# A graph network on one Trainium2 core: node tiles in edge order five quarter steps later, the first block of edges ahead of the order checks, and all source one-hots of the first stage on ScalarE

## The chip, the cores and the metric

The kernel runs on one core of a Trainium2 chip. A core has five engines with instruction queues of their own: PE (TensorE, matrix products; the profile shows its weight loads apart, as PEld), DVE (VectorE), ACT (ScalarE), POOL (GpSimd) and SP (SyncE, which issues DMAs here). The metric is the device time of one execution in microseconds. The kernel before took 5880.89 us (median of 3 runs, 5874.62 to 5888.94).

## The reference

There are 12,500 nodes with 96 features and 200,000 edges, sorted by destination. Four layers follow each other, each with a residual and a layer norm:

- layer 0: `x @ W_self + (mean over incoming edges of x[src]) @ W_neigh + b`
- layer 1, twice: `concat(x @ W1 + b1, sum over incoming edges of (x @ W0 + b0)[src]) @ W2 + b2`, divided by the row's standard deviation
- layer 2: attention per edge with 8 heads, `exp(clip(sum(K[src] * Q[dst] * E)))`, where E comes from 96 features of the edge itself, and a weighted mean of `V[src]`
- layer 3: a softmax over incoming edges of `relu(x[src])`, the weighted sum, and a product with W

So the core of the work is done four times without attention (layer 0, layer 1 twice, layer 3): take a row of a node table for each edge's source, and sum the rows by destination.

## The kernel before

The nodes make 98 tiles of 128 (NB). The edges, in their given order, make 1563 edge tiles of 128. Since the edges are sorted, each node tile draws its edges from a short stretch of some 32 edge tiles. A check in the kernel falls back to a general version if the data don't fit; it plays no part here.

**Two ways to sum.** For the first NS = 72 node tiles (60 in layer 3, NS3) the edges are rearranged: for a destination tile `d`, each edge gets a place by its source tile, 25 granules of 128 places (SQ). The rows of a granule are taken from the node table, which stays in SBUF, by four matmuls against a one-hot by source (`ohT`, L1366; L1231 in the first stage), copied out of PSUM as `msg` (L1369; L1235), and summed by a matmul with a one-hot by destination (`ohd`, L1375; L1244). For the other node tiles (26, or 38 in layer 3) the edges stay in their order: POOL fetches their rows from DRAM with indirect DMAs of 128 rows, one for each edge tile (L1311 in `by_edges`), and PE sums them with a one-hot over 32 edge tiles (L1297). A few edges per node tile that found no place go to two spare granules, whose rows POOL fetches as well (L1175, L1184). In the text an *item* is one granule of one node tile, so a pass over 72 node tiles has 1800 items.

**Stages in time** (us in the profile): a prologue to about 75; the node tables of layer 0 and the first block of edges to about 250; the first stage to 1636, in which the places are worked out, the one-hots made and stored, and layer 0 summed, all together; two passes of layer 1 to 2257 and to about 2900; attention to 4985; the pass of layer 3 to the end.

**The prologue and the first stage.** `edge_constants` makes constants and then checks the order of the edges: first and last destination of each edge tile (`c.first`, `c.cont`, `c.same`), and whether edges are out of order (`c.loose`). `edge_block` loads a block of 128 edge tiles (BL) and works out a few columns per edge; its last value, `b.lead`, compares with `c.first`. `edge_steps` takes 64 edge tiles at a time (GE): a scan per 16 edge tiles counts edges of the same source tile (L1018), a product and 16 small matmuls collect the counts (L1022, L1024), and then one-hots A and R and 64 matmuls put the edges in their places (L1076 to L1097). `l0_nodes` makes the table of layer 0 in 25 batches. `first_sums` is a generator that `passes` resumes: at its step for tile `d` it asks for the places as a row over all partitions (`ask_row`, `bc`), makes the one-hots by source (`one_hots`, L1143 to L1156) and by destination (`destinations`, L1137), fetches the spare rows, and runs the items of the tile. Odd tiles have their source one-hots made by ACT, a square and a ReLU on halves; even tiles by DVE, one comparison.

**A pass** (`whole_pass`) goes through the items in order, ten (or five) at a time: gather on PE, copies on ACT and DVE, then the sums of the ten before. Between them it resumes `by_edges` by quarter steps, four for each node tile in edge order. How often is set by one line (L1390):

```
while made * len(items) < i * 4 * (NB - ns):
    next(others)
    made += 1
```

Inside, each quarter step asks POOL for the rows of edge tiles up to 16 units of four ahead (13 in layer 3), and the first quarter step of the next node tile sums the one before (`take`):

```
while at < min(4 * d - 9 + k + deep, units):
    ...
if k == (3 if count else 0) and d > ns:
    take(d - 1)
```

The first quarter step of a pass therefore asks for nine units, 36 edge tiles, at once. The spare rows of two node tiles are fetched by one more DMA on the same POOL queue, four node tiles ahead (`ask_spares`).

**What sets the order.** Outside attention a planner orders each engine's instructions when the kernel is built, from the program's order and its own costs; an engine then works through its list in order. In attention the order is written out by hand. So where the text says "built order", it means the list of instructions on an engine as the built kernel has it.

Of the kernel before, what the change touches and what calls it, by code (L numbers as in the profile page):

```python
# [11 lines left out]
F32 = mybir.dt.float32  # L12
# [3 lines left out]
AF = mybir.ActivationFunctionType  # L16
ALU = mybir.AluOpType
AX = mybir.AxisListType
PSUM = bass.MemoryType.PSUM
# [4 lines left out]
P = 128  # L24
# [6 lines left out]
NB = 98  # L31
# [487 lines left out]
SD = SQ * P  # L519
# [3 lines left out]
BL = 128  # L523
# [18 lines left out]
def gnn_fast(  # L542
# [4 lines left out]
    nc = tc.nc  # L547
# [12 lines left out]
    pcol1 = const.tile([P, 1], F32, name="pcol1")  # L560
    nc.vector.tensor_scalar(pcol1, pcol, 1.0, None, op0=ALU.add)
    less = const.tile([P, 1], F32, name="less")
# [73 lines left out]
    with tc.tile_pool(name="w_work", bufs=2) as work, tc.tile_pool(name="w_psum", bufs=2, space=PSUM) as psum:  # L636
        for i in range(DEPTH):
            t = const.tile([D + 1, 2 * D], F32, name=f"w_l1_{i}")
            for k, (w, b) in enumerate(((W1[i], b1[i]), (W0[i], b0[i]))):
# [3 lines left out]
                c = work.tile([D, D], F32, name="wc")  # L643
# [187 lines left out]
    def edge_constants(big):  # L831
        c = Edges()
# [17 lines left out]
        c.run = None  # L850
        c.placed = []
        c.blocks = {}
        with tc.tile_pool(name="s_ord", bufs=1) as ordp, tc.tile_pool(name="s_ordp", bufs=2, space=PSUM) as psum:
            ones_f = ordp.tile([P, P], F32, name="ones_f")
            nc.vector.memset(ones_f, 1.0)
# [23 lines left out]
            for j0 in range(0, NT, 512):  # L879
                n = min(512, NT - j0)  # L880
# [10 lines left out]
            o = ordp.tile([P, 2, rw], I32, name="o")  # L891
# [14 lines left out]
            p = psum.tile([P, 512], F32, name="p")  # L906
            nc.tensor.matmul(p[:, :1], ones_f, c.loose, start=True, stop=True)
            nc.vector.tensor_scalar(c.loose, p[:, :1], 0.5, None, op0=ALU.is_ge)
        return c

    def edge_block(c, blk, psum, b0):

        nb = min(BL, NT - b0)
# [42 lines left out]
        b = c.blocks[b0] = Edges()  # L956
# [4 lines left out]
        nc.vector.tensor_copy(col, p[:, : 2 * P].rearrange("p (k t) -> p k t", k=2))  # L961
        hi_i = blk.tile([P, 2, BL], I32, name="hi_i", bufs=1)
        nc.vector.tensor_scalar(hi_i, col, 7, None, op0=ALU.arith_shift_right)
        hi = blk.tile([P, 2, BL], F32, name="hi", bufs=1)
        nc.vector.tensor_copy(hi, hi_i)
        b.shi = blk.tile([P, BL], BF16, name="shi")
        nc.vector.tensor_copy(b.shi, hi[:, 0, :])
# [25 lines left out]
        nc.vector.tensor_add(b.j, b.j, q)  # L993
        b.more = blk.tile([P, BL], F32, name="more")
        nc.vector.tensor_scalar(b.more, q, -1.0, float(SQ - 1), op0=ALU.mult, op1=ALU.add)
        b.lead = blk.tile([P, BL], F32, name="lead")
        nc.vector.tensor_tensor(b.lead[:, :nb], hi[:, 1, :nb], c.first[:, b0 : b0 + nb], op=ALU.is_equal)

    def edge_steps(c, work, psum, t0):

# [2 lines left out]
        b = c.blocks[t0 - c0]  # L1003

        pr = psum.tile([P, 3, GE], F32, name="pr")
        for i0 in range(0, n2, CH):
            n = min(CH, n2 - i0)
# [19 lines left out]
        n = n2  # L1027
# [18 lines left out]
        cs = slice(c0, c0 + n)  # L1046
        at = small("at_")
        nc.vector.tensor_mul(at, full[:, :n], c.cont[:, t0 : t0 + n])
        nc.vector.tensor_mul(at, at, b.lead[:, cs])
        nc.vector.tensor_add(at, at, pr[:, 1, :n])  # L1050
        none = small("none")
        nc.vector.scalar_tensor_tensor(none, at, float(SPARE), ovf, op0=ALU.is_ge, op1=ALU.mult)
# [91 lines left out]
    def one_hots(work, d, bc):  # L1144

        o = work.tile([P, SD], FP8, name="ohT0", bufs=2)
        if d % 2:

            for c in range(0, SD, SD // 2):
                b = bc[:, c : c + SD // 2]  # L1150
                nc.scalar.activation(b, b, AF.Square, bias=less)
                nc.scalar.activation(o[:, c : c + SD // 2], b, AF.Relu, bias=1.0, scale=-1.0, saturate=False)
        else:
            nc.vector.tensor_scalar(o, bc, pcol1, None, op0=ALU.is_equal, saturate=False)
        nc.sync.dma_start(ohT_d[d], o)
        return o  # L1156

# [167 lines left out]
    def whole_pass(of, table, done, rest_done, at=None):  # L1325

        ns = of[0]
        W = table.shape[1]
        R = 4 * D // W
        items = [(d, q) for d in range(ns) for q in range(SQ)]  # L1330
        got, acc = {}, {}
        with ExitStack() as c2:
            tabp = c2.enter_context(tc.tile_pool(name="e_tab", bufs=1))
            work = c2.enter_context(tc.tile_pool(name="e_work", bufs=2))
            msgp = c2.enter_context(tc.tile_pool(name="e_msg", bufs=4))
            psum = c2.enter_context(tc.tile_pool(name="e_psum", bufs=1, space=PSUM))
            at = at or load_table(tabp, table)
            sp = {}

            def ask_spares(d):  # L1340
                if d < ns:
                    sp[d] = sp[d + 1] = gather_spares(tabp, table, d)

            ask_spares(0)
            ask_spares(2)
            others = by_edges(of, msgp, psum, work, table, rest_done, 16 if W == 2 * D else 13)
            next(others)
            made = 0

            def fetch(d):  # L1350
                if d < ns:
                    if d % 2 == 0:
                        ask_spares(d + 4)
                    got[d] = reload(work, d)

            def gather(now, banks, engine):

                n = len(now) // R
                ps = psum.tile([P, n, 512], F32, name=f"rows{n}", bufs=n)
                m = msgp.tile([P, n, R * W], F16, name=f"msg{n}")  # L1360
                for i, (d, q) in enumerate(now):
                    if q == 0:
                        fetch(d + 1)
                    for j in range(NG):
                        a, b = granule(at, got[d][0], sp[d], q, j, d % 2)
                        nc.tensor.matmul(  # L1366
                            ps[j * GR : (j + 1) * GR, i // R, i % R * W : (i % R + 1) * W], a, b, start=True, stop=True
                        )
                (nc.scalar.copy if engine else nc.vector.tensor_copy)(m, ps[:, :, : R * W])  # L1369
                return [(d, q, m[:, i // R, i % R * W : (i % R + 1) * W]) for i, (d, q) in enumerate(now)]  # L1370

            def scatter(d, q, m):
                if q == 0:
                    acc[d] = psum.tile([P, 512], F32, name="acc", bufs=2)
                nc.tensor.matmul(acc[d][:, :W], got[d][1][:, q, :], m, start=(q == 0), stop=(q == SQ - 1))  # L1375
                if q == SQ - 1:
                    done(work, psum, d, acc.pop(d))
                    got.pop(d)
                    sp.pop(d)

            fetch(0)
            waiting = []
            for i in range(0, len(items), 5 * R):
                now = []
                for b0, b1, scalar in ((0, 1, True), (1, 3, True), (3, 5, False)):
                    now += gather(items[i + b0 * R : i + b1 * R], b1 - b0, scalar)
                for w in waiting:
                    scatter(*w)
                waiting = now
                while made * len(items) < i * 4 * (NB - ns):  # L1390
                    next(others)
                    made += 1
            for w in waiting:
                scatter(*w)
            for _ in others:
                pass
# [360 lines left out]
    def passes():  # L1757
        with ExitStack() as c1:
# [8 lines left out]
            nc.scalar.dma_start(q_d[:QM], none[:QM])  # L1767
            nc.scalar.dma_start(q_d[QM + NB * P :], none[: P - QM])
            with ExitStack() as c2:
                tabp = c2.enter_context(tc.tile_pool(name="f_tab", bufs=1))  # L1770
                spare["ring"] = spares(tabp, 2 * D, F16, "spare")
                blk = c2.enter_context(tc.tile_pool(name="s_blk", bufs=2))
                step = c2.enter_context(tc.tile_pool(name="s_work", bufs=2))
                work = c2.enter_context(tc.tile_pool(name="f_work", bufs=1))
                msgp = c2.enter_context(tc.tile_pool(name="f_msg", bufs=2))
                psum = c2.enter_context(tc.tile_pool(name="f_psum", bufs=1, space=PSUM))
                pieces, at = new_table(tabp, 2 * D, F16)
                nodes = l0_nodes(work, psum, pieces)
                sums = first_sums(work, msgp, psum, at, tabs_d[0], c.placed, in_batches(l0_stage, count=True))
                next(sums)  # L1780
                others = by_edges(
                    rest, msgp, psum, work, tabs_d[0], in_batches(l0_stage, count=True, name="sums_e"), 11, count=True
                )
                made = 0
                turn = 1 - AHEAD
                for k, t0 in enumerate(range(0, TS, GE)):
                    if t0 == 0:
                        edge_block(c, blk, psum, 0)
                    if t0 % BL == 0 and t0 + BL < TS:
                        edge_block(c, blk, psum, t0 + BL)  # L1790
                    edge_steps(c, step, psum, t0)
                    for _ in range(26):
                        next(nodes, None)

                    while turn <= min(4 * k, NS - 2):
                        next(sums)
                        turn += 1
                        while made * NS <= turn * 4 * (NB - NS):
                            next(others)
                            made += 1  # L1800
                for _ in sums:
                    pass
                for _ in others:
                    pass
                for b0 in range(-(-TS // BL) * BL, NT, BL):
                    edge_block(c, blk, psum, b0)
# [85 lines left out]
```

## Time and profile before

| | |
|---|---|
| median of the runs | 5880.89 us |
| the profiled execution, its own time | 5885.37 us |
| its span, first to last instruction | 5883.6 us |
| PE busy | 4446.7 us (76%), granted clock 0.749 on the mean |
| DVE busy | 4378.5 us (74%) |
| ACT busy | 2718.9 us (46%) |
| POOL busy | 4095.9 us (70%) |
| moved by DMA | 920.46 MB, 156 GB/s |

A busy time is the share of the span in which an engine had an instruction at work; issuing a DMA isn't counted, except for POOL's indirect DMAs. An average over the span mixes stages with different limits, so the views that matter are those by stage and in a window. In a row of a timeline the columns are start, duration, engine, line and operation, and in brackets the idle time before it and what ended it. In a row of waits: who waited for what, us in total, how often, the longest.

### The profile page before, as it was taken

The page shows a single profiled execution, that of the slowest core. Times are in us where ns is not written, and L with a number is a line of the kernel's source. Part 1 is how long each engine was busy: PE and PEld are TensorE (multiplying, and loading weights), DVE is VectorE, ACT ScalarE, POOL GpSimd, SP SyncE. Part 2 cuts the span into 40 slices and gives each one's busy share as a digit, 9 for nine tenths or more (in the row PEclk, how much of TensorE's full clock was granted, in tenths as well). Part 3 has the DMA queues.
Part 4 walks back from the last instruction along what each step waited for, and adds up shares of the span by engine and source line. Part 5 has one row for each costly group of instructions (what it writes and reads, how often), then busy time and mean ns, then how long its engine had stood idle before and what let it go on. Part 6 is the DMA issues. An engine that isn't in the chain of part 4 may idle for free. (4 is left out here: it accounts for less than half of the span.)

```text
span 5883.6 us, 131235 instructions
## 1 busy us (share of the span) xinstructions
PE 4446.7 (76%) x51487; PEld 3267.7 (56%) x51487; DVE 4378.5 (74%) x9063; ACT 2718.9 (46%) x5380; POOL 4095.9 (70%) x3648
## 2 busy tenths in 40 slices
PE   4667777777778987898666667666666765899998
PEld 3444444554456765666566566666666664445454
DVE  7589899998746665776677777777777777577776
ACT  1445444444534443555444444444444444444444
POOL 0267677767667775777477777777777776777773
PEclk7576767776779998999755655555556566899999
DMA  3555555555556665776555555555555554555553
GB/s 100 156 156 184 172 170 173 164 166 166 179 149 167 171 160 140 190 193 187 150 152 155 157 156 156 156 156 155 156 153 156 155 157 131 137 145 151 146 151 88
DMA packets 671708, 920.46 MB, mean 156 GB/s; under 512 B 399034, under 2 KB 465293, under 8 KB 671077
## 3 DMA queue, kind: packets, MB, share of 16 engines
q1 hardware_dynamic: 502198, 621.59, 33.7%
q0 software_dynamic: 150624, 283.99, 20.8%
q10 hardware_dynamic: 18255, 6.39, 0.5%
q8 instruction: 406, 6.65, 0.5%
q14 instruction: 225, 1.84, 0.1%
HBM read 778.75 MB, written 132.81 MB: 155 GB/s over the span
## 5 line engine op out<-in xcount | busy, mean ns | idle before, releaser
L1311 POOL DMA_INDIRECT rows_e<-tab_d,cols x1257 | 1658.3, 1319 | 423.7 <-issue 292.9
L1536 POOL DMA_INDIRECT kv<-kv_d,cols x1563 | 1590.9, 1018 | 485.4 <-issue 382.0
L1369 ACT CAST msg<-rows 128x768 f16<-128x768 f32 (+1 forms) x1320 | 796.9, 640 | 853.8 <-PE rows L1366 832.8
L1629 PE MATMUL acc<-mh,ohe 128*128 128x208 f16 x3115 | 566.7, 355 | 661.3 <-DVE ohe L1613 653.8
L1369 DVE CAST msg<-rows 128x768 f16<-128x768 f32 x660 | 630.0, 955 | 369.5 <-PE rows L1366 363.6
L1629 PEld LDWEIGHTS <-ohe 128*128 128x128 bf16 x3115 | 379.3, 137 | 781.8 <-DVE ohe L1613 738.4
L1366 PE MATMUL rows<-tab,ohT 128*32 128x192 f16 (+1 forms) x19992 | 763.8, 277 | 56.0 <-ACT msg L1369 21.7
L1311 POOL DMA_INDIRECT rows_e<-ex_d,cols x611 | 592.2, 969 | 186.2 <-issue 154.2
L1375 PE MATMUL acc<-msg,ohd 128*128 128x192 f16 (+1 forms) x5100 | 693.7, 276 | 1.6 <-issue 1.6
L1574 PE MATMUL ep<-w_e,attr 97*128 97x96 f32 x3126 | 689.7, 396 | 5.0 <-DVE s L1582 4.2
L1574 PEld LDWEIGHTS ep<-w_e,attr 97*128 97x128 f32 x3126 | 660.4, 310 | 14.1 <-DVE s L1582 4.6
L1366 PEld LDWEIGHTS <-ohT 128*32 128x32 fp8e4 x19992 | 425.5, 97 | 350.8 <-issue 298.5
L1297 PE MATMUL acc<-rows_e,ones_e 128*128 128x192 f16 (+2 forms) x3660 | 493.3, 285 | 93.8 <-DMA rows_e<-tab_d,cols 51.2
L1582 DVE TENSOR_TENSOR s<-ep,kv 128x384 f32<-128x384 f32 x391 | 217.6, 556 | 442.8 <-DMA kv<-kv_d,cols 358.9
L1594 ACT ACTIVATE ex<-sc 128x32 f32<-128x32 f32 x391 | 89.6, 229 | 984.8 <-DVE sc L1586 951.8
L1375 PEld LDWEIGHTS <-ohd 128*128 128x128 fp8e4 x5100 | 407.0, 99 | 233.4 <-issue 179.3
L1235 ACT CAST msg<-rows 128x768 f16<-128x768 f32 x600 | 366.0, 641 | 319.0 <-PE rows L1231 293.0
L1297 PEld LDWEIGHTS <-ones_e 128*128 128x128 bf16 x3660 | 365.2, 117 | 187.9 <-issue 93.9
L1244 PE MATMUL acc<-msg,ohd 128*128 128x193 f16 x1800 | 305.1, 295 | 112.8 <-ACT msg L1235 100.6
L1231 PE MATMUL rows<-tab,ohT 128*32 128x192 f16 x7056 | 332.2, 294 | 49.6 <-ACT msg L1235 20.0
L1175 POOL DMA_INDIRECT spare<-tab_d,spare_i x72 | 141.5, 1966 | 317.8 <-DMA rowd<-lorow 134.9
L1018 DVE TENSOR_TENSOR_SCAN cnt<-cb,run,sb 128x2048 bf16<-128x2048 bf16 (+1 forms) x73 | 324.3, 4443 | 4.6 <-DMA cb<-crow 4.6
(701 smaller groups left out, 7577.7 us busy)
## 6 DMA issues: line engine op xcount, KB each, us to landing
ohT<-ohT_d SPq DMA_DIRECT2D x204, 400.0 KB
ohd<-ohd_d SPq DMA_DIRECT2D x204, 400.0 KB
attr<-cols_edge_attr_dram SPq DMA_DIRECT2D x390, 192.0 KB
bc<-rowd SPq DMA_DIRECT2D x72, 800.0 KB
qb<-qrow SPq DMA_DIRECT2D x97, 512.0 KB
sb<-srow SPq DMA_DIRECT2D x72, 512.0 KB
cb<-crow SPq DMA_DIRECT2D x72, 512.0 KB
ohd_d<-ohd SPq DMA_DIRECT2D x72, 400.0 KB
```

The source lines that it names most:

```text
L1018: nc.vector.tensor_tensor_scan(cnt[:, : n * P], cb[:, : n * P], sb[:, : n * P], c.run, op0=ALU.mult, op1=ALU.add)
L1231: nc.tensor.matmul(ps[j * GR : (j + 1) * GR, i // R, i % R * W : (i % R + 1) * W], a, b, start=True, stop=True)
L1235: nc.scalar.copy(m[:, : n * R, :W].rearrange("p (b r) w -> p b r w", r=R), ps[:, :n, : R * W].rearrange("p b (r w) -> p b r w", r=R),)
L1244: nc.tensor.matmul(acc[d][:, : W + 1], got[d][1][:, q, :], m, start=(q == 0), stop=(q == SQ - 1))
L1297: nc.tensor.matmul(acc[:, : W + count], ones[:, :, i], rows_of[u][:, i, : W + count], start=(t + i == first), stop=(t + i == last),)
L1311: nc.gpsimd.indirect_dma_start(out=m[:, i, :W], out_offset=None, in_=table, in_offset=bass.IndirectOffsetOnAxis(ap=rest_src[:, t : t + 1], ...
L1366: nc.tensor.matmul(ps[j * GR : (j + 1) * GR, i // R, i % R * W : (i % R + 1) * W], a, b, start=True, stop=True)
L1369: (nc.scalar.copy if engine else nc.vector.tensor_copy)(m, ps[:, :, : R * W])
L1375: nc.tensor.matmul(acc[d][:, :W], got[d][1][:, q, :], m, start=(q == 0), stop=(q == SQ - 1))
L1536: nc.gpsimd.indirect_dma_start(out=kv[:, i, :], out_offset=None, in_=kv_d, in_offset=bass.IndirectOffsetOnAxis(ap=cols[:, t0 + i : t0 + i ...
L1574: nc.tensor.matmul(ep[:, i, :], a[:, i * P : (i + 1) * P], w_e, start=True, stop=True)
L1629: nc.tensor.matmul(acc[d].rearrange("p t w -> p (t w)"), ohe[:, k * P : (k + 1) * P, i], m[:, i].rearrange("p t w -> p (t w)"), start=(t = ...
```

## The change

Three things are changed.

1. In `whole_pass` the quarter steps of `by_edges` start when five of them would have been made, and are spread over the rest of the pass so that they end where they did.
2. The checks of the order leave `edge_constants` for a function of their own, `edge_orders`, which `passes` calls after `edge_block` has been issued for the first block. For this `b.lead` moves into `edge_steps`, which makes it for its 64 edge tiles, and `hi` is kept in two buffers.
3. In the first stage ACT makes the one-hots by source of all 72 tiles, each in five pieces of 640 columns instead of two of 1600.

```diff
     def edge_constants(big):
...
+        return c
+
+    def edge_orders(c, big):
         with tc.tile_pool(name="s_ord", bufs=1) as ordp, tc.tile_pool(name="s_ordp", bufs=2, space=PSUM) as psum:
...
-        hi = blk.tile([P, 2, BL], F32, name="hi", bufs=1)
+        hi = blk.tile([P, 2, BL], F32, name="hi")
+        b.hi = hi
...
-        b.lead = blk.tile([P, BL], F32, name="lead")
-        nc.vector.tensor_tensor(b.lead[:, :nb], hi[:, 1, :nb], c.first[:, b0 : b0 + nb], op=ALU.is_equal)
...
-        nc.vector.tensor_mul(at, at, b.lead[:, cs])
+        lead = small("lead")
+        nc.vector.tensor_tensor(lead, b.hi[:, 1, cs], c.first[:, t0 : t0 + n], op=ALU.is_equal)
+        nc.vector.tensor_mul(at, at, lead)
...
-        if d % 2:
-
-            for c in range(0, SD, SD // 2):
-                b = bc[:, c : c + SD // 2]
-                nc.scalar.activation(b, b, AF.Square, bias=less)
-                nc.scalar.activation(o[:, c : c + SD // 2], b, AF.Relu, bias=1.0, scale=-1.0, saturate=False)
-        else:
-            nc.vector.tensor_scalar(o, bc, pcol1, None, op0=ALU.is_equal, saturate=False)
+
+        for c in range(0, SD, SD // 5):
+            b = bc[:, c : c + SD // 5]
+            nc.scalar.activation(b, b, AF.Square, bias=less)
+            nc.scalar.activation(o[:, c : c + SD // 5], b, AF.Relu, bias=1.0, scale=-1.0, saturate=False)
...
-                while made * len(items) < i * 4 * (NB - ns):
+
+                while (made + 5) * len(items) < i * (4 * (NB - ns) + 5):
...
             with ExitStack() as c2:
+                blk = c2.enter_context(tc.tile_pool(name="s_blk", bufs=2))
+                step = c2.enter_context(tc.tile_pool(name="s_work", bufs=2))
+                with tc.tile_pool(name="b_psum", bufs=1, space=PSUM) as psum:
+                    edge_block(c, blk, psum, 0)
+                edge_orders(c, big)
                 tabp = c2.enter_context(tc.tile_pool(name="f_tab", bufs=1))
                 spare["ring"] = spares(tabp, 2 * D, F16, "spare")
-                blk = c2.enter_context(tc.tile_pool(name="s_blk", bufs=2))
-                step = c2.enter_context(tc.tile_pool(name="s_work", bufs=2))
...
-                    if t0 == 0:
-                        edge_block(c, blk, psum, 0)
                     if t0 % BL == 0 and t0 + BL < TS:
                         edge_block(c, blk, psum, t0 + BL)
```

More of the change, by code (lines that the diff above doesn't have):

```diff
@@ L908, in edge_constants @@
             nc.vector.tensor_scalar(c.loose, p[:, :1], 0.5, None, op0=ALU.is_ge)
-        return c
     def edge_block(c, blk, psum, b0):
```

## The prediction

> **What bounds the kernel now.** I read the busy time by stage first. Columns: PE, PEld, DVE, ACT, POOL busy us (instructions), granted PE clock, DMA share, GB/s.
>
> ```profile
> 75.00:250.00 175.00, 109.78 (x479) 88.65 (x479) 112.50 (x247) 61.80 (x278) 3.46 (x5) 0.55 0.52 146
> 250.00:1550.00 1300.00, 956.09 (x11639) 626.50 (x11640) 1158.69 (x2189) 618.38 (x980) 949.45 (x479) 0.70 0.54 169
> 1636.00:2257.00 621.00, 513.06 (x10113) 410.93 (x10105) 372.67 (x786) 271.10 (x533) 443.24 (x457) 0.91 0.58 154
> 2257.00:2905.00 648.00, 546.59 (x10121) 404.64 (x10121) 436.69 (x959) 310.70 (x683) 452.94 (x460) 0.93 0.66 178
> 2905.00:4985.00 2080.00, 1408.08 (x9363) 1276.09 (x9367) 1558.75 (x3422) 1006.97 (x2123) 1588.06 (x1560) 0.59 0.56 153
> 4985.00:5884.00 899.00, 838.50 (x9001) 416.68 (x9001) 630.70 (x1215) 405.29 (x708) 621.08 (x641) 0.96 0.50 137
> ```
>
> In the first stage (250 to 1550) DVE is busy 89%. In the last pass PE is (93%). In the two L1 passes no engine looks full, so I read POOL's and PE's timelines at a pass's start (last pass here), then PE's waits in the first L1 pass.
>
> ```profile
> 4999.38 0.95 POOL L1311 DMA_INDIRECT rows_e<-ex_d,cols  x1 [0.30 <-PE rows L1366]
> 5000.63 0.95 POOL L1311 DMA_INDIRECT rows_e<-ex_d,cols  x1 [0.31 <-issue]
> ```
> ```profile
> 5010.98 1.63 PE L1297 MATMUL acc<-rows_e,ones_e 128*128 128x384 f16 x9
> 5013.27 0.32 PE L1297 MATMUL acc<-rows_e,ones_e 128*128 128x384 f16 x1 [0.67 <-DMA rows_e<-ex_d,cols]
> ...
> 5041.18 0.48 PE L1297 MATMUL acc<-rows_e,ones_e 128*128 128x384 f16 x1 [0.72 <-DMA rows_e<-ex_d,cols]
> ```
> ```profile
> PE rows L1366 <- DMA spare<-tab_d,spare: 43.5, 9, 9.0
> PE acc L1297 <- DMA rows_e<-tab_d,cols: 28.8, 33, 1.6
> ```
>
> PE takes up its first edge-order tile and then runs at POOL's pace, a gather each 1.25 us (0.95 busy, 0.30 issue), for 25 to 31 us. POOL never pauses in a pass: in the first L1 pass 419 rows and 36 spares go out from 1640.3 to 2220.7, 1.276 us each. So PE waits there again, nine times, for spare rows queued behind them: POOL sets that pass.
>
> **What the Trainium skill says.** "TensorE: Matmul & The Clock Gate", Specifications (engine queue depth): ScalarE, VectorE and GpSimd queues are strict FIFO; the trace agrees, message copies stand behind one-hots (at 704.8 to 710.7 ACT runs 5.9 us of them). "DMA: Bandwidth & Descriptors", Issuing engine by pattern: indirect DMAs belong to GpSimd; here all 1.25 us of them sit on POOL.
>
> **Part 1, later node tiles.** The take-up of the first edge-order tile moves from item 80 to item 160 of 1800 in the L1 passes, and from 45 to 95 of 1500 in the last (an item is one granule of 128 edges); later ones come each 66 (before 69) or 38 items. But the number of POOL DMAs stays 455 or 641, and POOL starts when it did; only their order changes (four spares instead of three ahead, then fewer rows before the next). So what a pass gains is what POOL lets through.
>
> First L1 pass: PE's last wait ends at 2197.1, on the spare of node tile 66, POOL's 434th DMA (1640.3 + 434 x 1.276 = 2194.1, then 3 us to land). PE's end is 2237.7, 40.6 later. In the changed kernel's built order it is the 431st: 3 x 1.276 = 4 us earlier. Second: last wait 2772.8, spare 60 (396th), then 90.2 us for 276 items, 0.327 each. Spare 60 becomes 383rd, but spare 66 stays 434th: 2255.4 + 434 x 1.292 + 3 = 2819.1 with 126 items left (41.2): 2860.3 against 2863.0, 3 us. I take -4 and -3; bounds 0 (POOL as it is; no DMA is added, so no loss) and -15 each (PE ends 17 to 20 us after POOL's last gather).
>
> Last pass: PE reaches item 95 at 5011.0 + 50 x 0.37 (5 items in 1.85) = 5029.5. The 32nd row is POOL's 36th DMA: 4995.6 + 36 x 1.273 + 3 = 5044.4, so PE is through at 5045. Before, it is through item 45 at 5041.6 and at item 95 at 5060: 15 us. Rows 33 to 48 land at 5066 where PE would be done at 5063, minus 3: -12 to -13. After that both go 21.3 us per tile. Bounds -5 and -25 (whole stall). Passes together: -20.
>
> **Part 2, one-hots.** The rows (columns: busy us, mean ns | idle):
>
> ```profile
> L1154 DVE TENSOR_SCALAR ohT<-bc,pcol 128x3200 fp8e4<-128x3200 bf16 x32 | 60.8, 1901 | 1.5 <-DMA bc<-rowd 1.5
> L1151 ACT ACTIVATE bc<-bc,less 128x1600 bf16<-128x1600 bf16 x64 | 102.9, 1631 | 39.8 <-DMA bc<-rowd 39.6
> L1152 ACT ACTIVATE ohT<-bc 128x1600 fp8e4<-128x1600 bf16 x64 | 96.6, 1534 | 8.6 <-PE rows L1231 7.3 <-DVE nom_i L988 0.8 <-ACT lorow L1117 0.3
> ```
>
> DVE loses 36 x 1.88 = 68 us. ACT's pieces of 640 are in no trace: by "ScalarE: Activation LUTs", What ACT_TABLE_LOAD costs, an ACTIVATE with a pointer bias takes 280 + 0.833N ns, with immediates 186 + 0.833N, and they overlap by 93 in a row. For 1600 that is 1613 and 1519; the trace says 1631 and 1534. For 640 an estimate of 813 and 719, so 5 x 1.532 - 10 x 0.093 = 6.7 us a tile, where halves take 6.1. ACT gains 72 x 6.7 - 36 x 6.1 = 263 us, on 663 of 1386: 67%, by load hidden behind DVE. By order it isn't: message copies wait in ACT's queue. In the built orders I summed the other ACT work beyond 1 us between successive message copies: 212 us before, 328 after, +116 (often the five Relus in one row, 3.2 us). Before, PE waited 100.6 us for messages; taking 40 as the plain handshake (some 90 waits of 0.35 to 0.5), 60 of 212 showed, 28%. So +33 on PE, half on the path, +16; bounds 0 and +116.
>
> **Part 3, the first block early.** At the end of the table phase the built DVE order has placed 8 groups of 16 edge tiles instead of 4: four times A 1.22, oq 0.57, two R 0.57 and small ones, and one group more of scan 4.47, product 1.21 and compare 0.75: 25 us drawn out of the stage that DVE bounds into one where it is 64% busy. The price: on SP the loads and stores of blocks 0 and 1 and the first eight sb and cb loads now stand ahead of the first node rows, which were asked for at 7.5 us, and they wait for block 1's chb, ahead of which DVE has some 19 us more than it had; its idle time before (17 us in 0 to 75) absorbs little, since it waits there for weights. ACT's and POOL's queues get nothing new there. Nodes start later: +17; bounds +5 and +22. The 18 small compares for lead replace 8 of 0.28: +1, dropped.
>
> First stage: DVE's 68 + 25 = 93 us at three quarters (DVE already idles 11%, for PE's place matmuls and ACT's squares): -70, +17, +16 = -37. Sum -37 - 20 = -57 on the profiled 5885.4: 5828. The median of the runs is 4.5 lower: 5824. Attention (2080 us) keeps its written order: 0.
>
> **Rivals.**
> A, DVE alone paces the first stage (its 89% speaks for it, PE's 344 idle us against): -93/0.89 + 17 = -87, with -20: 5774.
> B, the initial stalls (22.5, 16.8, 18.6 us of waits for rows) go whole; POOL's unbroken queue speaks against: -58 instead of -20, 5786.
> C, ACT's blocks eat DVE's relief: first stage 0, passes -20: 5861. For it: 73% PE busy beside 89% DVE, coupled by two-deep buffers.
> D, slower: ACT paces the first stage, at L1235's copies behind five-piece one-hots. If 60% of the 116 shows (+70), half of the 70 relief is lost (-35), +17, -20: +32, 5913. It decides from the point where more than (70 + 20 - 17)/116 = 63% shows with all relief, or 33% with half of it. Against: 28% showed before.
>
> **How the numbers follow.** Mine 0.35 (own range 5800 to 5848, part terms between their bounds), A 0.25, B 0.10, C 0.17, D 0.13. 0.2% is about what can be told from no change, 12 us: below 5869 faster. Mine, A, B and 0.10 of C: 0.80; the rest of C and a little of D: same 0.09; D 0.11. From A's far side (16 us for nodes on time) to C's upper part the range is 5758 to 5886, which leaves out most of D and a tail of A.
>
> **What would show it.** Right: the waits for rows_e at a pass's start shrink to about 15 us in the last pass; in the first L1 pass waits for spares grow by about what those for rows lose, and POOL's 580 us stay. DVE's busy time falls by 65 to 70 and ACT's rises by some 260; the first stage ends near 1600 with waits of PE for messages above 130 us; the first x transposes come near 92 instead of 75. Wrong: the L1 passes shorten by over 15 us each (POOL isn't the bound), or the first stage moves by over 80 or not at all.

## The result, and the profile after

The changed kernel takes 5880.1 us (median of 12 runs, 5869.37 to 5886.75), the kernel before 5880.62 (12 runs, 5874.41 to 5888.94): ratio 0.9998, 95% interval 0.9990 to 1.0006. The forecast was 5824. The 57 us that it expected aren't there.

The profiled execution of after is the fastest of its twelve (5869.37, span 5867.5). So its stretches add up to 16 us less than those of before, where the medians differ by half a microsecond; the other 15 are scatter between executions, which one profile doesn't place. The view of busy time by stage, for after (window, its length, then PE, PEld, DVE, ACT and POOL busy with instructions, granted PE clock, DMA share, GB/s):

```profile
99.00:260.00 161.00, 116.57 (x529) 94.52 (x529) 106.12 (x263) 63.49 (x287) 3.93 (x5) 0.60 0.48 134
...
260.00:1652.00 1392.00, 1040.69 (x12296) 650.56 (x12300) 1128.78 (x2218) 926.28 (x1623) 852.01 (x495) 0.68 0.55 170
1652.00:2265.60 613.60, 515.22 (x10113) 410.97 (x10112) 374.18 (x786) 272.18 (x533) 439.64 (x457) 0.92 0.59 156
2265.60:2914.00 648.40, 555.36 (x10121) 410.64 (x10121) 438.22 (x959) 310.52 (x683) 450.26 (x459) 0.92 0.65 178
2914.00:4989.00 2075.00, 1413.58 (x9359) 1281.08 (x9359) 1559.52 (x3422) 1007.02 (x2123) 1583.37 (x1560) 0.59 0.56 154
4989.00:5868.00 879.00, 831.39 (x9001) 417.46 (x9001) 630.36 (x1215) 404.97 (x708) 618.60 (x641) 0.97 0.52 140
```

The same view of before, for the whole of the first stage:

```profile
254.00:1636.00 1382.00, 1011.16 (x12370) 661.36 (x12371) 1205.58 (x2304) 660.41 (x1055) 977.25 (x496) 0.71 0.56 172
```

The load moved as forecast: in the first stage DVE is busy 77 us less and ACT 266 us more. But the stage is some 10 us longer, and DVE's idle time in it went from 176 to 263 us. One of the forecast's own signs of being wrong, a first stage that does not move, came. In the next table a stretch begins where the named instruction first starts in the trace; "iota once" is a variant explained with the experiments.

| stretch from | before | after | change | forecast | iota once | change |
|---|---|---|---|---|---|---|
| start of the span | 74.9 | 98.9 | +24.0 | +17 | 97.7 | +22.8 |
| first node transpose | 178.8 | 161.6 | -17.2 | | 165.8 | -13.0 |
| first gather matmul, first stage | 1382.1 | 1391.4 | +9.3 | -70 +16 | 1352.6 | -29.5 |
| first gather matmul, first L1 pass | 621.4 | 613.7 | -7.7 | -4 | 618.2 | -3.2 |
| first gather matmul, second L1 pass | 644.0 | 644.8 | +0.8 | -3 | 644.5 | +0.5 |
| first gather of attention | 2083.7 | 2078.9 | -4.8 | 0 | 2080.1 | -3.6 |
| first gather matmul, last pass, to the end | 898.6 | 878.2 | -20.4 | -13 | 880.3 | -18.3 |
| span | 5883.6 | 5867.5 | -16.1 | -57 | 5839.2 | -44.4 |

The passes did what was forecast. The first take-up of an edge-order tile in the last pass, on PE in after (start, duration, and the wait in brackets):

```profile
5033.33 4.06 PE L1297 MATMUL acc<-rows_e,ones_e 128*128 128x384 f16 x24
5037.77 0.32 PE L1297 MATMUL acc<-rows_e,ones_e 128*128 128x384 f16 x1 [0.37 <-DMA rows_e<-ex_d,cols]
...
5046.41 0.80 PE L1297 MATMUL acc<-rows_e,ones_e 128*128 128x384 f16 x2 [1.80 <-DMA rows_e<-ex_d,cols]
```

24 of the 32 rows are there when PE comes, where before it found 9. It is through at 5047, with the pass starting 4.3 us later than before; its waits for rows add up to 6.4 us there, where the forecast had about 15. In the waits of PE in the first L1 pass of after (us, times, longest), spares cost 18 us less than before and rows 6 us more:

```profile
PE acc L1297 <- DMA rows_e<-tab_d,cols: 34.8, 43, 1.9
PE rows L1366 <- DMA spare<-tab_d,spare: 25.5, 8, 9.8
```

ACT's pieces of 640 columns have a row now, in the groups of after by form (busy us, mean ns | idle):

```profile
L1153 ACT ACTIVATE bc<-bc,less 128x640 bf16<-128x640 bf16 x360 | 284.7, 826 | 25.2 <-DMA bc<-rowd 24.1 <-ACT lorow L1120 0.3 <-DVE s__12541 L1124 0.3
L1154 ACT ACTIVATE ohT<-bc 128x640 fp8e4<-128x640 bf16 x360 | 243.0, 729 | 17.5 <-PE rows L1231 12.6 <-issue 2.5 <-DVE cnt L1019 0.7
```

**Where the first stage stands still.** Two rows of waits were not in the profile of before at this size. DVE's and then PE's in the first stage of after:

```profile
DVE nom_i L991 <- POOL nom_i L990: 22.9, 3, 11.0
```
```profile
PE pr L1025 <- DVE cnt L1023: 101.7, 28, 18.5
```

Before, DVE waited 0.3 us for `nom_i`, and PE 61.5 for `cnt`. `nom_i` is a small counter that `edge_block` has POOL make by an iota, once for each block of 128 edge tiles; the next DVE instruction shifts it. Here is the longest of the three stand-stills in the timeline of after, on POOL, DVE, PE and ACT:

```profile
1159.91 4.36 POOL L1311 DMA_INDIRECT rows_e<-tab_d,cols  x1 [0.30 <-issue]
...
1181.92 0.94 POOL L1311 DMA_INDIRECT rows_e<-tab_d,cols  x1 [0.30 <-issue]
1182.87 0.25 POOL L990 IOTA nom_i<- 128x128 int32 x1
```
```profile
1171.97 0.16 DVE L1450 RECIPROCAL dg<-dg 128x4 f32<-128x4 f32 x1
1183.16 0.23 DVE L991 TENSOR_SCALAR nom_i<-nom_i 128x128 int32<-128x128 int32 x1 [11.03 <-POOL nom_i L990]
```
```profile
1175.93 0.35 PE L1231 MATMUL rows<-tab,ohT 128*32 128x192 f16 x8
1194.77 0.59 PE L1025 MATMUL pr<-ones_b,cnt 128*128 128x1 bf16 x16 [18.49 <-DVE cnt L1023]
```
```profile
1180.20 1.34 ACT L1154 ACTIVATE ohT<-bc 128x640 fp8e4<-128x640 bf16 x2
1193.62 0.52 ACT L760 ACTIVATE sq<-centred 128x384 f32<-128x384 f32 x1 [12.07 <-DVE centred L758]
```

An iota of 0.25 us stands in POOL's queue behind fifteen gathers. DVE has finished all that precedes its shift at 1172.1 and waits 11 us. Behind the shift in DVE's queue are, among others, a one-hot, a scan and the product `cnt`. PE's next instruction needs that `cnt`, so PE stops for 18.5 us, with gathers that could have run behind it; ACT, which has one-hots to make until 1181.5, runs dry as well. And nothing needs the shift yet: its result is first read by this instruction of DVE, 168 us later:

```profile
1350.94 0.22 DVE L993 TENSOR_SCALAR nom<-nom_i 128x128 f32<-128x128 int32 x1
```

### The profile page after: what moved, and what is told of

Same layout as the page of the kernel before. It is cut to its first block, busy times and chain, and to the rows that moved or that the text cites. A ratio compares the mean times of both kernels' runs of the same rounds, so it can differ in the third digit from the quotient of the medians.

```text
span 5867.5 us, 131577 instructions
## 1 busy us (share of the span) xinstructions
PE 4494.1 (77%) x51487; PEld 3275.7 (56%) x51487; DVE 4317.4 (74%) x9036; ACT 2985.8 (51%) x5956; POOL 3954.7 (67%) x3648
## 5 line engine op out<-in xcount | busy, mean ns | idle before, releaser
L1311 POOL DMA_INDIRECT rows_e<-tab_d,cols x1257 | 1536.1, 1222 | 513.4 <-issue 301.0
L1369 ACT CAST msg<-rows 128x384 f16<-128x384 f32 (+1 forms) x1320 | 796.7, 639 | 797.2 <-PE rows L1366 774.6
L1244 PE MATMUL acc<-msg,ohd 128*128 128x193 f16 x1800 | 343.6, 313 | 122.8 <-ACT msg L1235 120.0
L1231 PE MATMUL rows<-tab,ohT 128*32 128x192 f16 x7056 | 358.1, 311 | 7.7 <-ACT ohT L1154 4.2
```

The source lines that it names most:

```text
L1231: nc.tensor.matmul(ps[j * GR : (j + 1) * GR, i // R, i % R * W : (i % R + 1) * W], a, b, start=True, stop=True)
L1244: nc.tensor.matmul(acc[d][:, : W + 1], got[d][1][:, q, :], m, start=(q == 0), stop=(q == SQ - 1))
L1311: nc.gpsimd.indirect_dma_start(out=m[:, i, :W], out_offset=None, in_=table, in_offset=bass.IndirectOffsetOnAxis(ap=rest_src[:, t : t + 1], ...
```

## The experiments

Of the four chips that ran them, two took 7936 to 8083 us for the kernel before, two 5882 to 5883. The first twelve runs fell on the slower ones; each ratio is to the kernel before on the same chip, and stretches are compared with the tables above only for the last six. What is slow there is told at the end.

**The three parts, each alone.** Part 1 is the one line in `whole_pass`, part 2 the body of `one_hots`, part 3 all the rest of the diff.

> The kernel before with the first part alone (edge-order node tiles five quarter steps later). The forecast's step: first L1 pass -4, second -3, last pass -13, sum -20: 5861. As the profile of after reads (-8, 0, -20, with the first stage the same): -28: 5853. Rival, the start stalls only move to other places of the passes: within 5 of before, 5876 to 5886. The first stage should keep its 1382 us (from the first gathers at 254 to the first gathers of the first L1 pass at 1636).

> The first part alone once more, on a chip where the kernel before takes some 5880 if one is had. The forecast's step: -4, -3 and -13 in the three passes. As the profile of after reads: -8, 0, -20. If the start stalls only move, the passes keep 621, 606 and 872. First stage unchanged at 1382 within 10.

Measured 0.9980 (0.9969 to 0.9991) and 0.9985 (0.9972 to 0.9998), both on the slower chips: a gain of 12 to 16 us, less than the passes of after show. Part 1 on the faster chips is contained in the run with all one-hots on DVE below: its passes took 615.3, 644.8 and 881.6 us, so -6, +1 and -17; the first and the last lie in the ranges forecast, and the second a microsecond outside.

> The kernel before with the second part alone (all source one-hots of the first stage on ScalarE, in fifths). The forecast's step: DVE -68 at three quarters and +16 for later message copies, -35: 5846. Rival, ScalarE and PE pace the stage now: DVE's 68 us turn into waits of DVE for PE (ohd and ones_e for acc, 33 us before, above 80 then), first stage 0 to +15: 5881 to 5896. Rival, the change did gain in this part and the late start of the third lost it: below 5855.

> The second part alone once more. The forecast's step: first stage -35. ScalarE and PE pace the stage: first stage +5 to +25 (it was +0.5% of the whole on the slower chip), DVE's waits for acc (ohd and ones_e) from 33 to above 80, PE's waits for message copies above 100 as they were, ScalarE's waits for rows from 293 below 190.

> The second part alone. Leaving DVE's one-hots out gained 23 us of the first stage and leaving ScalarE's out 4, so by load alone: -23 for DVE and +5 for ScalarE: first stage 1364, ratio 0.997. If ScalarE's pieces delay the copies as on the slower chip: first stage 1395 or more, ratio above 1.002. The forecast's -35 would be a first stage of 1347.

Measured 1.0051 (1.0030 to 1.0072), 1.0061 (1.0044 to 1.0077), and on a faster chip 1.0039 (1.0025 to 1.0052): 23 us slower. This part isn't worth -35; it loses by itself. Its first stage on the faster chip:

```profile
251.40:1656.70 1405.30, 1054.75 (x12361) 655.81 (x12361) 1143.80 (x2268) 925.38 (x1627) 826.83 (x496) 0.68 0.55 169
```

1405 us where before has 1382. DVE waits 21.9 us in it for `nom_i`, and the longest of PE's waits for `cnt` has 13.4. So the late iota comes without the third part, too. But PE's waits for `cnt` add up to 53.5 us here, less than the 61.5 of before, so these stand-stills alone don't explain the loss.

> The kernel before with the third part alone (first block of edges ahead of the order checks). The forecast's step: DVE draws 25 us ahead (-19), nodes start 17 later: -2: 5879. Rival, the late start goes through in full (node transposes from 99 instead of 75) and nothing is drawn ahead that counts: +15 to +24: 5896 to 5905. Rival, the early places help by more than the start costs: below 5870.

> The third part alone once more. The forecast's step: -2, from -19 for work drawn ahead and +17 for later nodes. As the slower chip and the start of after read: first node transpose near 99 (+24), first gathers of the first stage +7, and the first stage shorter by what is drawn ahead, -5 to -20: sum -10 to +5.

> The third part alone. Theory: DVE and PE stand 36 us behind one iota again; it starts its first gathers 7 to 15 us later and draws work ahead: ratio 1.002 to 1.006. The forecast's -2: ratio 0.9997. If the stall is absorbed (as parts 1 and 3 with the iota made once say, 7 us faster only on the slower chip): ratio 0.998 to 1.001.

Measured 1.0006 (0.9996 to 1.0016), 1.0035 (1.0024 to 1.0047), and on a faster chip 1.0034 (1.0022 to 1.0046): 20 us slower. The last trace has the stand-still at its largest, on POOL, DVE and PE:

```profile
297.73 0.95 POOL L1314 DMA_INDIRECT rows_e<-tab_d,cols  x1 [0.30 <-issue]
...
333.92 0.95 POOL L1314 DMA_INDIRECT rows_e<-tab_d,cols  x1 [0.30 <-issue]
334.88 0.25 POOL L990 IOTA nom_i<- 128x128 int32 x1
```
```profile
296.00 0.14 DVE L1021 CAST run<-cnt 128x1 f32<-128x1 bf16 x1
335.17 0.23 DVE L991 TENSOR_SCALAR nom_i<-nom_i 128x128 int32<-128x128 int32 x1 [39.02 <-POOL nom_i L990]
```
```profile
300.60 0.51 PE L1234 MATMUL rows<-tab,ohT 128*32 128x192 f16 x8
336.61 0.59 PE L1025 MATMUL pr<-ones_b,cnt 128*128 128x1 bf16 x16 [35.50 <-DVE cnt L1023]
```

Thirty gathers at 1.25 us stand before the iota. The stage is 1386.9 us long with that wait in it, and its first gather matmul comes 13.6 us later than before: the sum is the 18 us that its end is late. That the wait costs its full 39 us is not shown by this; the pair of parts 1 and 3 below speaks against it.

**Pieces of another size, and parts 1 and 3 together.** Part 2 with `SD // 2` for `SD // 5`, and the changed kernel with the old body of `one_hots`.

> The second part alone, but with two pieces of 1600 columns instead of five of 640. If what costs is ScalarE's load (36 tiles x 6.1 = 220 us more instead of 263), it is 5 to 15 us faster than the fifths. If what costs is a message copy standing behind a piece (up to 1.6 us instead of 0.8), it is slower than the fifths by 5 to 30. If neither counts, it equals them within 5.

Measured 1.0063 (1.0046 to 1.0079) beside 1.0061 for the fifths: the size of the pieces makes no difference that shows.

> The changed kernel with the second part undone (odd tiles on ScalarE in halves, even tiles on DVE). If the parts add up and the forecast's terms for 1 and 3 hold: -20 - 2 = -22: 5859. If the second part cost nothing and gained nothing: the time of after, 5880. If the second part is what ate the gain of the first: -28 - 2 = -30: 5851. If the late start of the third ate it: 5873 or more.

Measured 0.9996 (0.9985 to 1.0008): no difference from before that shows, and 30 us faster than the changed kernel on slower chips (below). It has the stand-still of 36.6 us.

**The iota made once.** The counter is made in the prologue, and each block takes its own from it by an addition, so no block waits for POOL. With the iotas and shifts gone, the planner also orders the rest a little differently: instructions of DVE stand up to 91 places from where they stood in the changed kernel, nine in ten of them at most 9.

```diff
+        c.nom_i = big.tile([P, BL], I32, name="nom_i")
+        nc.gpsimd.iota(c.nom_i, pattern=[[1, BL]], base=8, channel_multiplier=0)
+        nc.vector.tensor_scalar(c.nom_i, c.nom_i, 4, None, op0=ALU.arith_shift_right)
...
-        nom_i = blk.tile([P, BL], I32, name="nom_i", bufs=1)
-        nc.gpsimd.iota(nom_i, pattern=[[1, BL]], base=b0 + 8, channel_multiplier=0)
-        nc.vector.tensor_scalar(nom_i, nom_i, 4, None, op0=ALU.arith_shift_right)
         nom = blk.tile([P, BL], F32, name="nom", bufs=1)
-        nc.vector.tensor_scalar(nom, nom_i, -1.0, float(SQ), op0=ALU.add, op1=ALU.mult)
+        nc.vector.tensor_scalar(nom, c.nom_i, float(b0 // 16 - 1), float(SQ), op0=ALU.add, op1=ALU.mult)
```

> The changed kernel as it is, beside its parts. If it behaves as in its first comparison: ratio 0.9998 to before. If the parts add as they measured alone (-0.2%, +0.6%, +0.1 to +0.35%): ratio 1.005 to 1.007. Its trace should again show DVE waiting for the iota of a block of edges (nom_i) behind POOL's gathers, 20 us or more in total, and PE waiting for the counts (cnt) right after.

> The changed kernel with the iota of a block of edges made once in the prologue, so that DVE's nom takes it from a constant and never waits for POOL (12 iotas and 12 shifts of 0.23 us are gone). Theory: in the trace of after, the whole core stands still behind these iotas, 11.5 and 18.5 us of PE's waits for cnt and a part of 8.3. If that ate the gain: 25 to 35 us faster than the changed kernel on the same chip. Rival, ScalarE and PE pace the stage and the stall only takes up their slack: within 8 of the changed kernel.

On a slower chip the changed kernel measured 1.0033 (1.0023 to 1.0042), and with the iota made once 0.9999 (0.9985 to 1.0013): 32 us faster, as expected. But the trace of the changed kernel there misses its expectation: DVE waits 7.4 us for `nom_i`, not 20 or more. The first stage is 37.9 us shorter without the iota all the same (1595.1 and 1557.2). So on that chip the stand-still is not what the gain came from, or not the most of it; what was stays open.

> Parts 1 and 3 (one-hots as before), with the iota made once. In the traces of part 3 alone and of parts 1 and 3, DVE stands 36.6 us for one iota queued behind 30 gathers at 301 to 338 us, and PE 37.8 us after it. Theory: that stall is what part 3 costs; without it 30 to 37 us faster than parts 1 and 3 (which were within 0.1% of before): ratio about 0.9955. Rival, the start of the nodes 24 us later is the cost and the stall is absorbed: ratio 0.999 to 1.000.

> Part 1 alone with the iota made once. In before and in part 1 alone DVE waits 0.3 us for the iotas, so nothing is to be had but 3 us of shifts: ratio 0.998, as part 1 alone (0.998 and 0.9985). If it gains 20 us or more, the order of the instructions moved and the theory of the stalls isn't tested by the two others alone.

Measured 0.9988 (0.9979 to 0.9998), 6 us better than parts 1 and 3 with their iota and not 30 to 37: a miss, with intervals that overlap. Part 1 with the iota made once came to 0.9982 (0.9971 to 0.9992), as part 1 alone, which had no wait to lose. On these chips one and the same first stage took 1600.7 us in one profile of part 1 and 1553.4 in another, so whole stages don't tell. But the same gather matmuls can be set side by side. Just behind the stall of parts 1 and 3 they come 35 us later, against the variant, than just ahead of it; 25 us further on the variant has given all but 7 of that back. It stands still on PE there:

```profile
339.84 0.34 PE L1234 MATMUL rows<-spare,ident_h 128*32 128x192 f16 x2 [12.55 <-DMA spare<-tab_d,spare_i]
```

POOL issued that fetch of spare rows at 337.12, behind the same gathers of edge rows. The rest goes in waits up to 359 us that the profile ascribes to ACT's copies, and those to no engine of this core. So without the iota PE soon waits for POOL's queue at another place, and the stall of 37 was worth little there.

> The changed kernel with the iota made once in the prologue, on a chip where the passes run as in the first two profiles, if one is had. Theory: the stand-still behind the iotas (8.2, 11.5 and 18.5 us of PE's waits for cnt in the profile of after) was added to the first stage: 20 to 35 us faster than after, ratio to before 0.994 to 0.9965, first stage about 1362. Rival, the stalls are absorbed: first stage 1385 to 1395, ratio 0.999 to 1.001.

On a faster chip: 5842.38 us (5838.42 to 5844.59), ratio 0.9929 (0.9916 to 0.9943), 40 us faster than before and, since the changed kernel equals before, than after too. It beats both. Its first stage, by busy time, and PE's wait for the counts in it:

```profile
263.50:1616.10 1352.60, 1039.73 (x12296) 652.81 (x12300) 1128.31 (x2212) 925.80 (x1622) 832.91 (x488) 0.67 0.56 175
```
```profile
PE pr L1025 <- DVE cnt L1023: 64.6, 22, 9.6
```

The stage is 38.8 us shorter than that of after, and this one row of waits is 37.1 us shorter (101.7 to 64.6). DVE, ACT and PE are busy for the same time within a microsecond. Set side by side by gather matmuls, the variant's lead steps up at each of the three stand-stills of after, by 3.9 us at 552, 8.3 at 1079 and 11.5 at 1183. In between it goes up and down (behind the last step between 20 and 49 us), as the two orders differ. So about 24 of the 39 us, by this estimate, are gained where DVE waited; the other 15 aren't traced to one wait.

**What relief is worth.** Three variants of before in which only the makers of the source one-hots change. In the first, even tiles take over the odd tile's one-hots; in the second the odd tiles take over the even tile's; both sum other rows, so they tell of time alone. The third is part 1 with every tile's one-hots on DVE.

```diff
+        if d % 2 == 0 and d:
+            o = last_oh[0]
+            nc.sync.dma_start(ohT_d[d], o)
+            return o
```
```diff
+        if d % 2:
+            o = last_oh[0]
+            nc.sync.dma_start(ohT_d[d], o)
+            return o
```
```diff
-        if d % 2:
...
-        else:
-            nc.vector.tensor_scalar(o, bc, pcol1, None, op0=ALU.is_equal, saturate=False)
+        nc.vector.tensor_scalar(o, bc, pcol1, None, op0=ALU.is_equal, saturate=False)
```

> The kernel before without DVE's source one-hots: each even tile (but the first) takes the one-hots of the odd tile before it, so the sums are other ones and only the time counts. DVE has 35 x 1.9 = 67 us less, ScalarE as before. The forecast's step (DVE's relief is worth three quarters): -50 in the first stage. Rival, DVE isn't what paces the stage any more than ScalarE and PE: -25 to +5. If it is -50, then ScalarE's added 263 us are what cost the second part (-50 to +45 is 95); if it is near 0, the forecast's relief never was there.

> The kernel before without ScalarE's source one-hots: each odd tile takes those of the even tile before it (other sums, the time alone counts). ScalarE has 36 x 6.1 = 220 us less, DVE as before. If ScalarE's load stands in front of message copies at the rate that the forecast took (28% of the blocks, half of it on the path), -15 to -30. If it costs as much per us as the second part's 263 us did (+45 and the DVE relief that was lost, 0.17 to 0.35 us per us): -40 to -75. If ScalarE has slack: 0 within 8.

> Part 1, and all source one-hots of the first stage on DVE (the opposite of the second part): DVE +36 x 1.9 = +68 us, ScalarE -220 us. If DVE paces the stage: +50 against part 1 alone, ratio 1.004. If ScalarE's pieces in front of the message copies pace it as much: -10 to -30 against part 1 alone, ratio 0.994 to 0.997, faster than before and after both. If they balance: ratio 0.998.

Measured 0.9962 (0.9949 to 0.9976), 0.9989 (0.9983 to 0.9996) and 1.0029 (1.0019 to 1.0038). Their first stages, in this order:

```profile
253.10:1612.20 1359.10, 1022.48 (x12362) 668.94 (x12361) 1143.81 (x2269) 664.10 (x1057) 911.29 (x496) 0.70 0.56 174
```
```profile
251.20:1629.30 1378.10, 973.42 (x12362) 667.03 (x12362) 1205.42 (x2305) 453.14 (x912) 1020.40 (x497) 0.71 0.55 173
```
```profile
253.60:1675.90 1422.30, 980.43 (x12364) 671.73 (x12365) 1269.08 (x2341) 454.33 (x912) 1009.91 (x497) 0.71 0.54 167
```

62 us less of DVE are worth 23 (one of its waits for `nom_i` has 7), 207 us less of ACT are worth 4, and 63 us more of DVE cost 40 although ACT has 206 less. So DVE does pace this stage, but relief returns some 0.37 us per us (0.48 if the wait of 7 is taken off), added load costs 0.63, and 0.75 is above both. Taking ACT's load away returns next to nothing.

**Why the iota became late.** The time from a block's iota on POOL to the DVE shift that uses it, for the last six blocks of the traces, in us:

| kernel | slack of each block |
|---|---|
| before | 115, 109, 150, 152, 145, 6 |
| after | 150, 0.3, 45, 171, 0.3, 0.3 |
| part 2 alone | 0.3, 17, 0.3, 28, 168, 0.3 |
| part 3 alone | 0.3, 115, 150, 152, 150, 108 |
| DVE's one-hots left out | 163, 37, 98, 0.3, 4, 7 |
| all one-hots on DVE | 113, 121, 123, 108, 111, 117 |

0.3 means that DVE stood there. Where DVE has the most to do, no iota has less than 108; where it is relieved, or has its blocks of edges earlier, some have nothing. But that isn't DVE's pace alone: the shift has another place in DVE's built order. In before, for five of these six blocks it stands right ahead of `nom`, the instruction that reads it (765.3 and 766.2 us for the second). In after it does so for two; the three on which DVE stood are started 89 to 168 us before their `nom`, and the one of part 3 alone 300 us (335.2 and 635.0). For the second block the shift is the 1222nd instruction that the profile counts on DVE in before and the 857th in after, while the iota went from the 198th to the 162nd on POOL. The planner pulled the shift forward by more than the iota. That it did so because it saw room on DVE, and took POOL's gathers for shorter than they are, is likely, but no run shows it.

## Why the prediction was wrong

**The failed step** is in the first stage, "-70, +17, +16 = -37", which has no term for DVE waiting on POOL. Part 3 sets it at nothing with "ACT's and POOL's queues get nothing new there", part 2 without a word. Nothing new was in POOL's queue, but something old was asked for sooner: the iotas. They were free in before because DVE came to their shifts 6 to 152 us after them. In the new built order three shifts stand far ahead of the instruction that reads them, and DVE stands 22.9 us behind POOL's gathers. The forecast read the built orders for message copies and places, and says nothing of where the shifts went. Making the iota once brought 38.8 us of the first stage and 40 of the whole: about 24 of them at the three stand-stills, the rest together with a changed order. From first gather to first gather the stage was forecast 54 us shorter and came out 9 longer; of these 63 us the iota accounts for 39, and the price of DVE's relief, below, for most of the rest.

**Part 1, -20**: right. The table has -27 in after, -21 with the iota made once, and the passes of the run with all one-hots on DVE make -22. In the last pass the forecast was through the first 95 items 15 us earlier; it was 17, and the 3 us that it took off again for the second tile weren't lost: that tile's rows were there. In the first L1 pass POOL kept its pace (from 1656.8 to 2233.4, 577 us) and the pass gained a few us, as argued. The sign that was named there, waits for spares growing as those for rows shrink, came the other way round.

**Part 2**: the pieces were sized well (estimate 813 and 719 ns, measured 826 and 729; ACT +266 us for 263), and DVE lost 62 us in part 2 alone and 17 in part 3 alone, for 68 and 25. "At three quarters" was mis-sized: leaving the work out returned 0.37 us per us. With that slope the 79 us that left DVE are worth 29, and the variant without the stall has -29.5 for the stage. That they agree so closely is in part luck, since the slope comes from one run that has a wait of 7 in it. Of the +33 for message copies on the row that the forecast read, PE's sums, 19 came: 100.6 us of waits before, 120.0 in after. But PE's gathers waited 17 us less, so together it is 120.6 and 123.5. Where ACT made no one-hots at all, the two together fell to 84.4 while the stage gained 4. So nothing shows that these waits lie on the path.

**Part 3**: node transposes came 24 us later, above the upper bound of 22. But the table phase then took 17 us less, so the first gathers were only 6.8 us late in after and 9.8 with the iota made once (13.6 in part 3 alone): "nodes start later +17" charged the delay in full where more than half was won back.

**The rivals.** C, "ACT's blocks eat DVE's relief", had the nearest number (first stage 0, passes -20), but by luck: with all of ACT's blocks in place and the iota made once, the stage is 29.5 us shorter. The same run speaks against D's pace-setting ACT. A (DVE alone, 5774) falls with the slope of 0.37. B, the start stalls whole, holds in the last pass alone, which became 17 to 20 us shorter, about the 18.6 of its stall.

With the measured sizes put in (+10 for the start, -30 for the stage, -21 for the passes) the steps make -41 for the variant without the stall, and 5842 was measured: -40. So no large term is missing there; it is no forecast. What stays open: part 2 alone is 23 us slower than before, while its load alone suggests -19 (-23 + 4), and its iota waits (21.9 us) are at most half of the 42 between. A rival for the rest is PE itself, busy 44 us longer than before in that stage (1054.75 against 1011.16) for the same matmuls; against it, 38 us less of PE, where ACT made no one-hots, came with a gain of 4. Part 2 was not run with the iota made once.

## What to carry to other kernels

When an engine is relieved, list what it takes from the other engines' in-order queues and how much slack each of those has in the trace: a slack that is used up turns up as a stand-still of everything queued behind. Then look in the new built order for consumers that stand long before their result is read. A tiny producer (here 0.25 us) doesn't belong in the queue of an engine that is filled with gathers of 1.25 us; make it once ahead of time or on the consumer. And before a relief is priced by an engine's busy share, one run with that work left out gives the slope.

## What the runs showed of the hardware that was not expected

**Gathers take longer under DVE's scans.** A gather, most often 0.95 us, took 4.36 us at 1159.91 while DVE ran a scan (1159.04, 4.48 us), and ended 0.8 us after the scan. Over the first stage of after, the 53 gathers that start while a long scan runs took 4.28 us on the mean and ended some 0.75 us after it; the other 434 took 1.43. The Trainium skill, "GPSIMD Engine Reference", 1. Specifications, says that POOL's SBUF interfaces are shared with VectorE and contend with DVE instructions that have two SBUF inputs; the scan has two, and the trace agrees. At 1159.91 it made the iota 3.4 us later still.

**PE's busy time is longer where ACT is fuller.** With the same matmuls (12291 to 12370 of them in the profiles of the first stage), PE was busy for 973 and 980 us where ACT makes no one-hots, 1000 to 1022 where it makes 36 tiles', and 1040 to 1055 where it makes all 72, at granted clocks of 0.71, 0.70 to 0.71, and 0.67 to 0.68. Why was not tested.

**The slower chips.** Their passes take 1.7 to 1.75 times as long (the last pass 1544.7 against 881.6 us), attention 1.2 times. PE's timeline in a pass on such a chip (part 1 alone):

```profile
1904.04 0.32 PE L1366 MATMUL rows<-tab,ohT 128*32 128x192 f16 x1 [1.08 <-issue]
1905.44 0.32 PE L1366 MATMUL rows<-tab,ohT 128*32 128x192 f16 x1 [1.08 <-issue]
1906.14 0.32 PE L1366 MATMUL rows<-tab,ohT 128*32 128x192 f16 x1 [0.38 <-issue]
```

Matmuls run one by one with pauses of 0.38, 1.08 or 1.79 us in which PE waits for nothing that the profile shows. Weight loads of that line idle 1509 us so in part 1 alone, and 299 in before on the faster chip. What holds them up there stays open.
